# Attention block with a spline FFN: key tile 0 of the later query tiles transposed by VectorE and moved by DMA

## The chip, the cores and the metric

One Trainium2 chip, one of its NeuronCores. The metric is the device time in microseconds of one execution. A core has TensorE (PE; its weight loads are listed as PEld), VectorE (DVE), ScalarE (ACT), GpSimd (POOL) and SyncE (SP). In this kernel SP computes nothing and issues most DMAs. Every engine works through its own instructions in the order of the program and waits on semaphores for the others.

## The reference

A block on x of shape 4 x 512 x 512 in float32: a layer norm, attention with 16 heads of 32 (ALiBi bias over the keys, causal mask), and an FFN whose weights are splines of control points. Both branches read the normalized x and are added to x.

```
xn = layernorm(x)
q, k, v = xn@Wq + bq, xn@Wk + bk, xn@Wv + bv            # 16 heads of 32
scores = q k^T / sqrt(32) + slope[h] * (key - 511)       # causal mask, softmax over keys
ctx = softmax(scores) v;  attn = ctx @ Wo + bo
gate, up = xn @ gate_w^T, xn @ up_w^T                    # weights: cubic splines of control points
out = x + attn + (silu(gate) * up) @ down_w^T
```

## The kernel before, in words

The kernel has an attention part, until about 371 us of the profile, and an FFN part behind it; the change lies in the first. Attention runs over 64 **units** (b, hg, i): batch b of 4, head group hg of 4 (four heads each), query tile i of 4 (128 queries each). Unit i sees the key tiles 0 to i. One loop over n issues the parts of several units, staggered: step n computes the scores of unit n, normalizes unit n-1, transposes and moves unit n-2 (`LAG_SWAP`), and turns unit n-3 (`LAG`) on TensorE. Since each engine runs in program order, the order of the loop body is the order on each engine.

For a unit:
- `scores` (L889, TensorE) writes four heads into PSUM banks; tiles 0 and 1 share one set of banks and are issued together when i is 0.
- `minima` (L907, VectorE) adds the bias table `dist` and finds each row's minimum; `exponentials` (L923, ScalarE) makes p and its sums; `normalize` (L936 reciprocal on VectorE, L938 scaling on POOL) divides p by the sums.
- The value product needs p with keys on the partitions. There are two ways to it. **Key tile 0**: `turn` (L951) transposes four heads on TensorE into PSUM, and ScalarE copies them to `pT` (L952). **Key tiles 1 to i**: `swap` (L964) transposes blocks of 32 x 32 on VectorE into `blocks`, and `move` sends the blocks to their partitions with four DMAs on SP's queue (L974), into `moved`. A block transpose leaves keys in steps of 4, so that k is stored in stepped order for the key tiles from 1 on (L844), while key tile 0 keeps its order (L843).
- `values` (L994), once per head group at n % 4 = 3, multiplies: four matmuls (four heads) for each key tile; key tile 0 from `pT` with 512 queries, key tile c from `moved` with 512 - 128c. `moved` has one buffer.

Between these lie the projections (`project` L826 for q and k, `value` L864, `proj` L490 for the output), placed at steps by the tables `items`, `small` and `early`, which also place `load_turned` (the next batch's x, 1 MB), `keep_samples` (1 MB to DRAM, by way of a queue `later` that is emptied at the end of each step, by `flush`), and layer norm pieces. VectorE also builds the FFN's weights in attention: a list `terms` of multiplications and additions (L1135) is worked off by a credit per step, `TERMS`; the tables that a term reads are loaded by `loads` (two DMAs of 512 KB, later 256 or 320 KB), which also go through `later`.

The end of step n is, in this order: `swap` on VectorE, terms, `items` and `small`, then

```
            move()
            flush()
```

so that SP's queue holds what the step's items issue, then the moves, then the late loads and samples.

Of the kernel before, what the change touches and what calls it, by code (L numbers as in the profile page):

```python
# [18 lines left out]
P = 128  # L19
B, S, D, H = 4, 512, 512, 16  # L20
HD = D // H
# [9 lines left out]
NSLOT = 7  # L31
# [21 lines left out]
TERMS = (0.7, 1.4, 1.4, 0.7)  # L53
# [347 lines left out]
def block_kernel(  # L401
# [46 lines left out]
    lone = [keep.tile([P, S], F32, name="lone0")]  # L448
# [20 lines left out]
    dist = wp.tile([P, NB * (NB + 1) // 2, P], F32, name="dist")  # L469
# [34 lines left out]
    def keep_samples(b):  # L504
        nc.sync.dma_start(
            out=samples[b][1 : D + 1].rearrange("(c p) s -> p c s", p=P), in_=xnT[b]
        )
        nc.sync.dma_start(out=samples[b][:1], in_=lone[0][:1])
        nc.sync.dma_start(out=samples[b][D + 1 : D + NW], in_=lone[0][: NW - 1])
# [77 lines left out]
    with ExitStack() as att:  # L587
# [19 lines left out]
        nc.gpsimd.memset(lone[0], 0.0)  # L607
# [13 lines left out]
        for i in range(NB):  # L621
            for c in range(i + 1):
                shape, steps = dist[:, i * (i + 1) // 2 + c], [[1, P]]
                if c:
                    shape = shape.rearrange("p (r y) -> p r y", y=Q32)
                    steps = [[1, NB], [NB, Q32]]
                nc.gpsimd.iota(
                    shape,
                    pattern=steps,
                    base=1 - S + (c + NB - 1 - i) * P,  # L630
                    channel_multiplier=0,
                    allow_small_or_imprecise_dtypes=True,
                )
                if c == i:
                    nc.gpsimd.affine_select(
                        out=shape,
                        in_=shape,
                        pattern=[[-step, n] for step, n in steps],
                        compare_op=ALU.is_ge,
                        fill=NEG,  # L640
                        base=0,
                        channel_multiplier=1,
                    )

        spare = feat[0].rearrange("p c h s -> p (c h s)")
        loads, terms = {}, []

        def row_terms():  # L650
            size = NB * 2 * P
            place = lambda n: (spare[:, (2 * n + k) * size :][:, :size] for k in range(2))
            shaped = lambda a: a.rearrange("p (q x n) -> p q x n", q=NB, x=2)
            parts = [(c, w) for c in range(TAPS) for w in range(2)]

            def load(n, queue=nc.sync):
                c, w = parts[n]
                tab, own = place(n % 2)
                queue.dma_start(out=tab, in_=coef[c])
                queue.dma_start(out=own, in_=rowpts[c, w])  # L660

            for n, (c, w) in enumerate(parts):
                to = wT[:, :, 2 * w : 2 * w + 2, :]
                tmp = shaped(wd[:, w * size : (w + 1) * size]) if c else to
                tab, own = (shaped(a) for a in place(n % 2))
                terms.append((1.2, tmp, tab, own, ALU.mult))
                if n + 2 < len(parts):
                    loads[len(terms)] = lambda n=n: load(n + 2)
                if c:
                    terms.append((1.2, to, to, tmp, ALU.add))  # L670
            return [lambda: load(0, nc.sync), lambda: load(1, nc.sync)]

        def down_terms():
            size = 5 * P
            at = np.cumsum([0] + [P * (hi - lo) * P for _, lo, hi, _ in DOWN_STEPS])

            def part(n, k):
                _, lo, hi, _ = DOWN_STEPS[n]
                return spare[:, (n % 3 * 2 + k) * size :][:, : (hi - lo) * P]

            def load(*steps):
                for n in steps:
                    for k, source in enumerate((downtab, downpts)):
                        given = source[at[n] : at[n + 1]].rearrange("(p x) -> p x", p=P)
                        nc.sync.dma_start(out=part(n, k), in_=given)

            loads[len(terms) - 1] = lambda: load(0, 1, 2)
            terms.append((2.4,))
            for n, (kind, lo, hi, c) in enumerate(DOWN_STEPS):
                to = (dR if kind == "v" else dM)[:, lo:hi].rearrange("p a n -> p (a n)")  # L690
                tmp = wd[:, n % 2 * size :][:, : (hi - lo) * P] if c else to
                terms.append((0.8, tmp, part(n, 0), part(n, 1), ALU.mult))
                if n + 3 < len(DOWN_STEPS):
                    loads[len(terms)] = lambda n=n: load(n + 3)
                if c:
                    terms.append((0.8, to, to, tmp, ALU.add))
# [120 lines left out]
        def project(name, b, hg, parts=1):  # L817
# [3 lines left out]
            def go(part=0):  # L821
                if part == 0:
                    ps.append(ps_m.tile([P, S], F32, name="mm"))
                tokens = slice(part * size, (part + 1) * size)
                for c in range(NB):
                    nc.tensor.matmul(  # L826
                        ps[0][:, tokens],
                        lhsT=wsb[name][:, c, hg * P : (hg + 1) * P],
                        rhs=xnT[b][:, c, tokens],
                        start=(c == 0),  # L830
                        stop=(c == NB - 1),
                    )
                if part < parts - 1:
                    return
                o = qkp.tile([P, S], F32, name=f"{name}T")
                g = slice(hg, hg + 1)
                if name == "q":
                    nc.scalar.activation(
                        o, ps[0], AF.Identity, bias=bqs[:, g], scale=qs[:, g]
                    )  # L840
                else:
                    g1 = bcol[:, 1, g]
                    nc.scalar.activation(o[:, :P], ps[0][:, :P], AF.Identity, bias=g1)  # L843
                    nc.scalar.activation(  # L844
                        o[:, P:].rearrange("p (t r y) -> p t r y", r=NB, y=Q32),
                        ps[0][:, P:].rearrange("p (t y r) -> p t r y", r=NB, y=Q32),
                        AF.Identity,
                        bias=g1,
                    )
                qk[b, hg, name] = o  # L850
# [25 lines left out]

        units = [(b, hg, i) for b in range(B) for hg in range(NHG) for i in range(NB)]
        soft, pT, banks = {}, {}, {}
        moved = {}
# [17 lines left out]
        def minima(u):  # L897
            b, hg, i = u
            nk = (i + 1) * P
            own = dist[:, i * (i + 1) // 2 :][:, : i + 1].rearrange("p c k -> p (c k)")  # L900
# [41 lines left out]
        def turn(u):  # L942
# [3 lines left out]
            if i == 0:  # L946
                pT[b, hg] = tp.tile([P, NG, S], F32, name="pT")
# [6 lines left out]
        def swap(u):  # L954
# [4 lines left out]
            if i == 1:  # L959
                moved[b, hg] = tp.tile([P, NB, NSLOT, NG, Q32], F32, name="moved")  # L960
            at = slice(2 * i - 2, 3 * i - 2)
            own = tp.tile([P, NB, i, NG, Q32], F32, name=f"blocks{i % 2}")
            for c in range(i):
                nc.vector.transpose(  # L964
                    own[:, :, c].rearrange("p r j k -> p j r k"),
                    soft[u][0][:, :, (c + 1) * P : (c + 2) * P].rearrange(
                        "p j (r k) -> p j r k", k=Q32
                    ),
                )
            to = moved[b, hg]  # L970

            def move():
                for a in range(NB):
                    nc.sync.dma_start(  # L974
                        out=to[:, a, at].rearrange("p s j k -> p (s j k)"),
# [5 lines left out]
        def values(b, hg):  # L981
# [3 lines left out]
            swapped = moved.pop((b, hg)).rearrange("p a s j k -> p s a j k")  # L985
            for c in range(NB):
                if c:
                    w = swapped[:, 3 * c - 3 : c + 4 : 2]
                    part = lambda j: w[:, :, :, j]
                else:  # L990
                    w = pT.pop((b, hg))
                    part = lambda j: w[:, j]
                for j in range(NG):
                    nc.tensor.matmul(  # L994
                        ps[j * HD : (j + 1) * HD, c * P :],
                        lhsT=vals[b][:, c, hg * P + j * HD : hg * P + (j + 1) * HD],
                        rhs=part(j),
                        start=(c == 0),
                        stop=(c == NB - 1),
# [26 lines left out]
        for b in range(B):  # L1026
# [16 lines left out]
            if b + 1 < B:  # L1043
                for t in range(NB):
                    small[at + 8 + t].append(lambda b=b, t=t: norm_turned(b + 1, t))
                items[at + (4, 5, 4)[b]].append(lambda b=b: load_turned(b + 1))
# [8 lines left out]
        for b in range(B):  # L1055
            at = 4 * NHG * b
            items[max(at - 4, 0)].append(lambda b=b: later.append(lambda: keep_samples(b)))
# [37 lines left out]
        done, credit = 0, 0.0  # L1095

        for n in range(len(units) + LAG):
# [4 lines left out]
            if u and u[2] == 0:  # L1102
                if old:
# [18 lines left out]
            if old and not (u and u[2] == 0):  # L1122
# [9 lines left out]
            while done < len(terms) and credit > 0.0:  # L1132
                cost, *term = terms[done]
                if term:
                    nc.vector.tensor_tensor(*term)  # L1135
                done += 1
                credit -= cost
                if done in loads:
                    later.append(loads[done])
# [3 lines left out]
            flush()  # L1143
            if n >= 12:
# [15 lines left out]
    lone.append(latep.tile([P, S], F32, name="lone1"))  # L1160
# [3 lines left out]
    def set_up_moments():  # L1164
        for zeros in (lone[1], *edge):
# [223 lines left out]
```

## Time and profile before

| | us |
|---|---|
| median of three runs | 526.22 (524.68 to 528.7) |
| the profiled execution, its own time | 524.87 |
| its span, first to last instruction | 523.1 |
| TensorE busy | 502.9 (96%) |
| VectorE busy | 349.5 (67%) |
| ScalarE busy | 285.9 (55%) |
| POOL busy | 243.5 (47%) |
| granted TensorE clock, mean | 0.993 |
| turns L951, busy of 256 matmuls | 41.3 |
| block transposes L964, busy of 96 | 61.8 |

DMA moves 104.88 MB, 201 GB/s on average. The profile is one execution; a busy share is an average over stages with different limits. A row of its groups names line, engine, operation, output and input tile, shape and count, then busy time and mean duration, then the engine's idle time just before these instructions and what ended it. In the timeline, rows merge neighbours: a start, a duration, and how many instructions (an f32 matmul counts as two, a transpose on TensorE as one).

### The profile page before, as it was taken

How to read it: one execution, taken by the hardware profiler on the slowest of the kernel's cores; microseconds unless marked ns; L12 is line 12 of the kernel's file. 1: busy time of each engine (PE TensorE's matmuls, PEld its weight loads, DVE VectorE, ACT ScalarE, POOL GpSimd, SP SyncE). 2: the span in 40 equal slices, each digit the busy share in tenths (PEclk: the TensorE clock that was granted, in tenths of full speed). 3: DMA queues.
4: the chain of work that ended last, by engine and by line, in shares of the span. 5: the costliest groups of instructions: out<-in, count | busy, mean ns of one | idle time of the engine just before them, and what ended most of it. 6: DMA issues, size and time to landing. Idle time of an engine off the chain costs nothing.

```text
span 523.1 us, 11781 instructions
## 1 busy us (share of the span) xinstructions
PE 502.9 (96%) x4092; PEld 246.2 (47%) x4092; DVE 349.5 (67%) x991; ACT 285.9 (55%) x774; POOL 243.5 (47%) x441
## 2 busy tenths in 40 slices
PE   7999899999999999999998999989899999999997
PEld 5644344444444444444434444434335646746462
DVE  6169888588778649968976456583233774856836
ACT  2377757666457656755765666775014523634232
POOL 3024636647446583745866547574036233231310
PEclk9999999999999999999998999998999999999999
DMA  8926887975797587768773436786747555654344
GB/s 304 338 104 165 276 233 213 271 212 161 234 312 215 147 248 190 211 194 255 198 237 93 117 79 175 218 214 163 250 142 232 178 207 181 245 196 146 138 160 166
DMA packets 65051, 104.88 MB, mean 201 GB/s; under 512 B 10368, under 2 KB 34944, under 8 KB 64480
## 3 DMA queue, kind: packets, MB, share of 16 engines
q1 hardware_dynamic: 60384, 95.73, 60.1%
q0 software_dynamic: 4608, 8.40, 5.5%
q8 instruction: 32, 0.52, 0.4%
q14 instruction: 27, 0.22, 0.2%
HBM read 54.27 MB, written 23.70 MB: 149 GB/s over the span
## 4 chain that ended last, share of the span: by engine, by line
PE 81%; DVE 7%; DMA 6%; SPq 4%; issue 2%; ACT 0%; DVEq 0%
PE mm L826 18%; PE g L570 9%; PE mm L864 8%; PE s L889 7%; PE mm L490 7%; PE c L994 6%; PE o L1261 6%; PE mm L951 5%; DMA moved<-blocks 4%; PE o L1207 4%; SPq L974 3%; PE o L1278 3%; PE o L490 3%; DVE p L907 3%; DVE blocks L964 2%; PE o L570 2%
## 5 line engine op out<-in xcount | busy, mean ns | idle before, releaser
L938 POOL TENSOR_SCALAR p<-p,inv 128x128 f32<-128x128 f32 (+3 forms) x256 | 146.5, 585 | 157.1 <-DVE inv L936 131.7
L923 ACT ACTIVATE p<-p,low 128x128 f32<-128x128 f32 (+3 forms) x256 | 140.6, 553 | 32.2 <-DVE low L907 32.2
L907 DVE CUSTOM_DVE_ANT_0 p<-s,dist 128x128 f32<-128x128 f32 (+3 forms) x256 | 108.7, 485 | 69.2 <-PE s L889 69.0
L1183 POOL COPY made<-inner 128x512 f32<-128x512 f32 x64 | 38.8, 635 | 101.0 <-DVE inner L1182 96.8
L964 DVE STREAM_TRANSPOSE blocks<-p 128x512 f32<-128x512 f32 x96 | 61.8, 682 | 4.0 <-POOL p L938 2.8
L1175 ACT ACTIVATE act<-g 128x512 f32<-128x512 f32 x60 | 31.0, 603 | 58.9 <-PE g L570 58.6
L570 PE MATMUL g<-feat,wT 32*64 32x512 f32 x832 | 61.8, 592 | 0.0
L864 PE MATMUL mm<-wv,xnT 128*128 128x512 f32 x128 | 57.9, 594 | 1.4 <-ACT xnT L777 1.4
L826 PE MATMUL mm<-xnT,wq 128*128 128x512 f32 (+1 forms) x136 | 57.9, 568 | 0.9 <-DVE xnT L813 0.9
L826 PE MATMUL mm<-xnT,wk 128*128 128x512 f32 (+1 forms) x136 | 58.0, 569 | 0.2 <-ACT xnT L777 0.2
L952 ACT COPY pT<-mm 128x512 f32<-128x512 f32 x64 | 36.8, 580 | 31.1 <-PE mm L951 31.1
L889 PE MATMUL s<-kT,qT 32*128 32x512 f32 (+3 forms) x512 | 52.0, 474 | 0.5 <-DVE low L907 0.3
L923 ACT ACTIVATION_READ_ACCUMULATOR p<-p,low 128x1 f32 x256 | 48.6, 190 | 0.0
L951 PE MATMUL mm<-ident,p 128*128 128x128 f32 x256 | 41.3, 286 | 0.0
L951 PEld LDWEIGHTS mm<-ident,p 128*128 128x128 f32 x256 | 28.5, 142 | 26.2 <-issue 18.9
L490 PE MATMUL mm<-ctxT,wo 128*128 128x512 f32 x88 | 39.8, 595 | 0.0
L1182 DVE TENSOR_TENSOR inner<-g,act 128x512 f32<-128x512 f32 x40 | 24.9, 684 | 21.7 <-PE g L570 15.5
L570 PEld LDWEIGHTS g<-feat,wT 32*64 32x64 f32 x832 | 29.3, 131 | 20.7 <-issue 9.7
L555 POOL DMA_DIRECT2D table<-samples x64 | 36.8, 581 | 0.0
L889 PEld LDWEIGHTS s<-kT,qT 32*128 32x128 f32 x512 | 21.3, 188 | 32.4 <-issue 15.4
L826 PEld LDWEIGHTS mm<-xnT,wq 128*128 128x128 f32 x136 | 24.9, 190 | 24.0 <-issue 22.0
L994 PE MATMUL c<-moved,v 128*32 128x384 f32 (+2 forms) x384 | 25.6, 402 | 10.6 <-DMA moved<-blocks 7.0
(113 smaller groups left out, 619.9 us busy)
## 6 DMA issues: line engine op xcount, KB each, us to landing
moved<-blocks SPq DMA_DIRECT2D x64, 192.0 KB
moved<-blocks SPq DMA_DIRECT2D x64, 128.0 KB
feat<-table SPq DMA_DIRECT2D x16, 512.0 KB
inner<-made SPq DMA_DIRECT2D x32, 256.0 KB
table<-samples POOLq DMA_DIRECT2D x64, 88.0 KB, 3.6
xp<-in_xp_dram SPq DMA_DIRECT2D x16, 256.0 KB
feat<-in_coef_dram SPq DMA_DIRECT2D x8, 512.0 KB
feat<-in_rowpts_dram SPq DMA_DIRECT2D x8, 512.0 KB
```

The costliest lines, as they stand in the source:

```text
L490: nc.tensor.matmul(ps, lhsT=wsb["o"][:, c, r * P : (r + 1) * P], rhs=ctxT[b][:, c, :], start=(c == 0), stop=(c == NB - 1),)
L570: nc.tensor.matmul(ps[k][cols, :], lhsT=wT[rows, q, 2 * w + part, cols], rhs=feat[b][rows, q, part, :], start=(part == 0), stop=(part == 1),)
L826: nc.tensor.matmul(ps[0][:, tokens], lhsT=wsb[name][:, c, hg * P : (hg + 1) * P], rhs=xnT[b][:, c, tokens], start=(c == 0), stop=(c == NB ...
L864: nc.tensor.matmul(ps[0], lhsT=xnT[b][:, c, t * P : (t + 1) * P], rhs=wsb["v"][:, c, :], start=(c == 0), stop=(c == NB - 1),)
L889: nc.tensor.matmul(banks[b, hg][j][:, at : at + (k + 1) * P], lhsT=qk[b, hg, "q"][rows, k * P : (k + 1) * P], rhs=qk[b, hg, "k"][rows, : ( ...
L907: nc.vector.tensor_tensor_reduce(out=p[:, j, :nk], in0=ps[j], in1=own, scale=-SLOPES[hg * NG + j], scalar=BIG, op0=ALU.add, op1=ALU.min, a ...
L923: nc.scalar.activation(p[:, j, :nk], p[:, j, :nk], AF.Exp, bias=low[:, j : j + 1], scale=-1.0, accum_out=total[:, j : j + 1],)
L938: nc.gpsimd.tensor_scalar(p[:, j, :nk], p[:, j, :nk], inv[:, j : j + 1], 1.0, ALU.mult, ALU.mult)
L951: nc.tensor.transpose(ps[:, j, :], p[:, j, :P], ident)
L964: nc.vector.transpose(own[:, :, c].rearrange("p r j k -> p j r k"), soft[u][0][:, :, (c + 1) * P : (c + 2) * P].rearrange("p j (r k) -> p ...
L994: nc.tensor.matmul(ps[j * HD : (j + 1) * HD, c * P :], lhsT=vals[b][:, c, hg * P + j * HD : hg * P + (j + 1) * HD], rhs=part(j), start=(c ...
L1183: nc.gpsimd.tensor_copy(made[:, k], four[:, k])
```

## The change

- `turn` is done for query tiles 0 and 1 alone (`TURNED = 2`). For tiles 2 and 3, key tile 0 goes the way of the others: one block transpose more on VectorE for each, and moves of three and four key tiles in place of two and three.
- k is stored stepped for all key tiles, with one activation in place of two. The rows of `pT` are then in stepped order, so its product needs v's first tile in the same order: `stepped(b)` copies it with four DMAs into a free slot of the moved tile, once per batch, at the step behind the last value product of the batch before.
- `values` has five groups of four matmuls in place of four: `pT` with 256 queries and the stepped v, then key tiles 0 to 3 from the moved blocks with 256, 384, 256 and 128 queries. The moved tile is now one tile, `blocks`, kept for the whole of attention.
- `dist` needs 4 tiles in place of 10. The zero rows for `samples` are issued by POOL at the start from a small buffer, not by SP in `keep_samples`.
- `keep_samples` goes two steps later, behind the moves of query tile 3, and `load_turned` to step 6 of its batch (it was at 4, 5, 4). Loads for terms are gathered in `due` and issued only at the end of steps with n % 4 of 1 or 2; a term whose load has not been issued waits. `TERMS` gives 0.9 in place of 0.7 at two of four steps, and an empty term of 2.4 is gone.

```diff
-NSLOT = 7
+NSLOT = 9
+TURNED = 2
-TERMS = (0.7, 1.4, 1.4, 0.7)
+TERMS = (0.9, 1.4, 1.4, 0.9)
...
-                    g1 = bcol[:, 1, g]
-                    nc.scalar.activation(o[:, :P], ps[0][:, :P], AF.Identity, bias=g1)
                     nc.scalar.activation(
-                        o[:, P:].rearrange("p (t r y) -> p t r y", r=NB, y=Q32),
-                        ps[0][:, P:].rearrange("p (t y r) -> p t r y", r=NB, y=Q32),
+                        o.rearrange("p (t r y) -> p t r y", r=NB, y=Q32),
+                        ps[0].rearrange("p (t y r) -> p t r y", r=NB, y=Q32),
                         AF.Identity,
-                        bias=g1,
+                        bias=bcol[:, 1, g],
                     )
...
+        blocks = tp.tile([P, NB, NSLOT, NG, Q32], F32, name="moved")
+        def stepped(b):
+            rows = vals[b][:, 0].rearrange("(y r) (a d) -> r y a d", r=NB, a=NB)
+            for r in range(NB):
+                to = blocks[r * Q32 : (r + 1) * Q32, :, 1]
+                nc.sync.dma_start(out=to.rearrange("p a j k -> p a (j k)"), in_=rows[r])
...
-            at = slice(2 * i - 2, 3 * i - 2)
-            own = tp.tile([P, NB, i, NG, Q32], F32, name=f"blocks{i % 2}")
-            for c in range(i):
+            first = int(i < TURNED)
+            at = slice(3 * i - 4 + first, 4 * i - 3)
+            own = tp.tile([P, NB, i + 1 - first, NG, Q32], F32, name=f"blocks{i % 2}")
+            for c in range(first, i + 1):
...
+            parts = [(lambda j: blocks[:, hg, 1, j], slice(0, TURNED * P), lambda j: turned[:, j])]
             for c in range(NB):
+                i = max(c, 1 if c else TURNED)
+                w = swapped[:, 3 * i - 4 + c : 6 + c : 3]
+                parts.append((head(vals[b][:, c]), slice(i * P, S), lambda j, w=w: w[:, :, :, j]))
...
-                items[at + (4, 5, 4)[b]].append(lambda b=b: load_turned(b + 1))
+                items[at + 6].append(lambda b=b: load_turned(b + 1))
...
-            items[max(at - 4, 0)].append(lambda b=b: later.append(lambda: keep_samples(b)))
+            items[at + 4 if b else 1].append(lambda b=b: stepped(b))
+            items[max(at - 2, 0)].append(lambda b=b: later.append(lambda: keep_samples(b)))
...
-                if old:
+                if old and old[2] < TURNED:
                     turn(old)
...
-            if old and not (u and u[2] == 0):
+            if old and old[2] < TURNED and not (u and u[2] == 0):
                 turn(old)
...
+            if n % NB in (1, 2):
+                for load in due.values():
+                    load()
+                due.clear()
```

## Prediction

> **What bounds the kernel now.** I read the page first: busy shares, then the chain that ended last.
>
> ```profile
> PE 502.9 (96%) x4092; PEld 246.2 (47%) x4092; DVE 349.5 (67%) x991; ACT 285.9 (55%) x774; POOL 243.5 (47%) x441
> PE 81%; DVE 7%; DMA 6%; SPq 4%; issue 2%; ACT 0%; DVEq 0%
> ```
>
> TensorE (PE) is busy for 96%, yet a fifth of the chain lies elsewhere, with VectorE (DVE), a move's issue (SPq) and a DMA in it. So there are two paths of nearly equal length. Next the groups by shape: the work that is removed or multiplied.
>
> ```profile
> L951 PE MATMUL mm<-ident,p 128*128 128x128 f32 x256 | 41.3, 286 | 0.0
> L964 DVE STREAM_TRANSPOSE blocks<-p 128x512 f32<-128x512 f32 x96 | 61.8, 682 | 4.0 <-POOL p L938 2.8 <-DMA moved<-blocks 1.2
> L952 ACT COPY pT<-mm 128x512 f32<-128x512 f32 x64 | 36.8, 580 | 31.1 <-PE mm L951 31.1
> ```
>
> Then TensorE's own waits, longest total first:
>
> ```profile
> PE c L994 <- DMA moved<-blocks: 7.0, 6, 2.9
> ```
>
> The only wait that returns (6 times, 2.9 us at most) is the value product's wait for the moves. I therefore measure the loop by a **window**, one for each of the 16 value products: from the end of the score matmuls of query tiles 0 and 1 to the first c<-moved matmul. Window 4 on TensorE's timeline (start us, us, instruction):
>
> ```profile
> 105.15 0.94 PE L889 MATMUL s<-kT,qT 32*128 32x128 f32 x16
> 106.02 0.66 PE L951 MATMUL mm<-ident,p 128*128 128x128 f32 x4
> ...
> 109.95 0.60 PE L951 MATMUL mm<-ident,p 128*128 128x128 f32 x4
> 110.39 3.60 PE L826 MATMUL mm<-xnT,wk 128*128 128x512 f32 x8
> ...
> 114.77 0.66 PE L951 MATMUL mm<-ident,p 128*128 128x128 f32 x4
> ...
> 120.02 1.06 PE L994 MATMUL c<-pT,v 128*32 128x512 f32 x8
> 120.90 1.48 PE L994 MATMUL c<-moved,v 128*32 128x384 f32 x24
> 122.31 0.66 PE L951 MATMUL mm<-ident,p 128*128 128x128 f32 x4
> ```
>
> It runs from 106.02 to 120.90, 14.88 us without a gap: the **TensorE path**. The **move path** starts at the same instant; DVE and SP timelines:
>
> ```profile
> 108.33 1.30 DVE L964 STREAM_TRANSPOSE blocks<-p 128x512 f32<-128x512 f32 x2
> 109.56 0.14 DVE L936 RECIPROCAL inv<-sum 128x4 f32<-128x4 f32 x1
> 109.61 1.86 DVE L964 STREAM_TRANSPOSE blocks<-p 128x512 f32<-128x512 f32 x3
> ```
>
> ```profile
> 109.66 5.65 SPq L974 DMA_DIRECT2D moved<-blocks  x8
> ```
>
> Two transposes for query tile 2, three for tile 3, eight issues of about 0.62 us. By the trace's packet records tile 2's packets (1024 B) start 4.85 to 8.15 us into the window, tile 3's (1536 B) 7.70 to 12.03; the last move has landed at 12.42. The product needs tile 3's four moves for every key tile, so this path has 14.88 - 12.42 = 2.5 us to spare. That spare is what the change spends.
>
> **TensorE's side.** Of four turns a head group, those of tiles 2 and 3 go. The start of the next matmul shows what a turn costs the stream: 0.44 (109.95 to 110.39) and 0.49 us (0.59 before the stretch product), though the busy column says 41.3 / 64 = 0.65; I take the gaps. Ahead of the moves' arrival the pT part has 256 columns in place of 512: 120.02 to 120.90 is 0.88, so 0.44 goes. An ordinary window shrinks from 14.72 to 14.72 - 0.44 - 0.49 - 0.44 = 13.35. Behind the arrival four matmuls of 256 columns are added: 0.44 plus some 0.03 for each extra group (122.31 - 120.90 = 1.41 for 768 columns), so 1.41 becomes 1.88, **+0.47, 16 times, +7.5 us**. If TensorE alone decided, 16 x (1.37 - 0.47) = 14.4 us would be gained.
>
> **The move path's side.** One transpose more for tile 2 and one for tile 3, each 61.8 / 96 = 0.62 to 0.64 us; DVE reaches both in order, so whatever stands between (reciprocal, term) is later too. The moves stay four DMAs a tile with as many packets, but of 1536 in place of 1024 B and 2048 in place of 1536 B. From first to last packet, 512-B moves take 2.4 to 3.6 us, 1024-B ones 2.9 to 3.4 where alone, 1536-B ones 4.1 to 4.9. So tile 2 grows by 0.7 to 1.5; I take 0.9. For tile 3 no move of 2048 B exists; lower bound 0 (four issues at 0.62 already pace 1.9 us; a gain is excluded, each packet being longer), upper 4.4 x 4/3 - 4.4 = 1.5; I take 1.0, the step from 1024 to 1536 B, the nearest row. In window 4 the two queues follow each other: 12.42 + 0.62 + 0.9 + 1.0 = **14.9 us** against TensorE's 13.35. The move path decides, with a wait of 1.5 us at the product; a term of 1.2 us between the transposes still hides behind tile 2's packets.
>
> [...]
>
> **The windows, before and after** (TensorE's timeline; after is the longer path):
> - Ordinary, 2, 3, 4, 7, 10, 12, 14: 15.27 + 15.87 + 14.88 + 15.98 + 14.88 + 14.73 + 14.72 = 106.3; after 7 x 14.9 = 104.3. **-2.0.** The waits of 0.96 and 1.07 in windows 3 and 7 came from `keep_samples`: its 1 MB stood in SP's queue right ahead of tile 3's moves (issued 90.00 and 179.32), and now goes two steps later, behind them.
> - 1 and 6, with over 2 us of small DVE work between the transposes: 16.78 + 14.73 = 31.5. In window 6 tile 3's packets begin at 9.15; less 0.35 for a shorter term, plus 1.24, plus 4.7 + 1.0 + 0.4 is 16.1; window 1 is like it, less its 1 MB of loads now behind the moves. After 32.0. **+0.5.**
> - 5 and 9, with four output projections (21.8 each): TensorE decides. **-2.7.**
> - 8, 13, 15, 16, with little TensorE work between, already on the move path: 8 and 13 grow by 0.62 + 0.9 + 1.0 = 2.5 each; in 15 and 16 tile 3's transposes wait for an output projection, so 0.62 + 1.0 each. **+8.2.**
> - 11: 18.94 with the 2.9 us wait behind `keep_samples` and a late xnT; after 14.9. **-4.0.**
>
> These cancel: 0.0.
>
> **The clock.** The granted clock falls after long waits:
>
> ```profile
> 260.00:280.00 20.00, 17.10 (x95) 7.79 (x97) 13.25 (x39) 12.70 (x38) 14.84 (x26) 0.93 0.64 191
> 340.00:360.00 20.00, 17.46 (x87) 7.70 (x86) 12.62 (x38) 12.14 (x38) 15.29 (x29) 0.91 0.72 194
> ```
>
> The last three columns are clock, DMA share, GB/s. Half clock came for 3.41 us after the waits of 2.90 and 2.54, not after 1.73; one such stretch costs 1.6 us (c, turn and s after 276.44 take 1.96, 1.12, 1.59 in place of 1.50, 0.66, 0.94). One goes with window 11, one may come with 2.6 us in windows 1 or 6: 0. [...]
>
> **Edits at nothing.** ScalarE loses 32 copies of 0.58 and one of two kT activations: idle there, 55% busy; nothing gained. DVE's 32 transposes are 20.6 us more; 69.0 us of waiting for s cover them outside the windows; uncovered, all 20.6. The zero rows' eight issues (0.58 each, the rows of POOL's table copies) go from SP to POOL, which does nothing before its first normalization at 28.34; uncovered, 4.6 us. The stepped v copy is four issues per batch (2.5 us), ahead of tile 2's moves in windows 5, 9 and 13, but the wait for the previous product ends some 8 us before window 13; uncovered, 2.5 there. Loads of tables now follow tile 3's moves; terms are the same operations, finished two head groups earlier. `load_turned` comes up to two steps later; its readers wait for `rows` as it is (2.2 us in all); late, it would hold DVE and the next q product by a few us.
>
> **The sum.** 0.0 + 7.5 + 0 = +7.5 on the profiled execution of 524.87 (span 523.1 and 1.8 around it): 532.4. The median shown, 526.22, lies 1.35 above that execution, so **533.5**.
>
> **Rivals.**
> - *Bytes ride free* (the other side): the larger moves pace by their issues, and only the transpose is added, 13.0, so TensorE's 13.35 decides. Ordinary windows lose 1.55 x 7, 1 and 6 1.9 each, 8 and 13 1.9 each, 15 and 16 1.0 each, 11 1.55: -22, so 511.5. For it: 512 and 1024 B differ little (2.4 to 3.6 against 2.9 to 3.4), and median packets are short (65 ns at 1536 B, mean 97). Against: 1536 B takes over a microsecond longer. It beats the old time once the move path is under 14.4.
> - *Half of it*: growth 0.95 in place of 1.9. About 14 windows are 0.95 shorter, -13: 520.5; with the forecast's side of it up to 528.
> - *More of it*: 15.6, the upper bound, since DMA is busy 0.7 to 0.85 in most of attention: +10, and with waits of 2.2 some half clocks, up to 550.
> - *VectorE becomes the bound*: 17 to 22 us busy per group of 18 to 28 now; if every added transpose lies on the path, 546. Against: its wait for s, 69.0.
>
> That the change misses its purpose is excluded: in the instruction order half the L951 turns are gone and DVE has 128 transposes.
>
> **How the numbers follow.** Forecast (moves at 14.6 to 15.3, 529 to 540) 0.45; bytes free 0.13; half 0.20; more 0.17; VectorE 0.05. A tenth of a microsecond in the move path is 1.4 us, so the range runs 522 to 545, the forecast's own 529 to 540. A measurement tells about 1% (5.3 us) from nothing; faster: 0.13 and 0.02 of half, 0.15; same: 0.18 of half and 0.16 of the forecast's lower end, 0.34; slower: 0.51.
>
> **What would show it.** Right: PE's busy time down by some 15 to 20 us while its waits "c <- DMA moved" rise from 7 to 20 us or more, in nearly every ordinary window; tile 3's packets 5 us or longer; no wait behind `keep_samples` in windows 3, 7, 11. Wrong: ordinary windows near 13.4 without a wait; tile 3's packets as short as now; waits of s for DVE in place of those of c.

## The result, and the profile after

The changed kernel takes 579.12 us (median of 6 runs, 575.23 to 580.56), the kernel before 525.72 beside it: ratio 1.101, 95% interval 1.097 to 1.105. The forecast was 533.5, with a range of 522 to 545: the sign was right, the size was not. The profiled execution took 576.13 us; its span is 574.4, which is 51.3 more than before, and that is what the tables below split up.

Busy shares and the chain that ended last, profile after:

```profile
PE 516.5 (90%) x4092; PEld 247.7 (43%) x4092; DVE 369.2 (64%) x1023; ACT 268.5 (47%) x726; POOL 242.6 (42%) x441
PE 62%; DMA 18%; SPq 9%; DVE 8%; issue 3%; ACT 0%; DVEq 0%
```

VectorE has 19.7 us more (20.6 were worked out). TensorE has lost half of its turns and gained as many product matmuls, and its busy time, which the forecast had falling by 15 to 20 us, *rose* by 13.6 us: the same matmuls took longer. Its idle time went from 20.2 to 57.9 us. The chain lies for 27% in DMA and its issue, against 10% before. Groups (busy, mean ns of one | idle before them):

```profile
L972 DVE STREAM_TRANSPOSE blocks<-p 128x512 f32<-128x512 f32 x128 | 80.9, 680 | 9.6 <-DMA moved<-blocks 8.0
L1000 PE MATMUL c<-moved,v 128*32 128x256 f32 (+2 forms) x512 | 42.2, 484 | 38.0 <-DMA moved<-blocks 17.4
L898 PE MATMUL s<-kT,qT 32*128 32x512 f32 (+3 forms) x512 | 60.0, 483 | 8.6 <-DVE low L916 8.6
```

VectorE's transposes wait 8.0 us for moves (1.2 before): tile 1 of the next head group writes the buffer that tile 3's moves still read. The product now waits 38.0 us in all (10.6 before). The profile names the transfer that came last, so this is spread over several rows of TensorE's waits (us, times, longest):

```profile
PE c L1000 <- DMA moved<-blocks: 17.4, 7, 3.9
PE s L898 <- DVE low L916: 8.6, 5, 2.6
PE c L1000 <- DMA xt<-in_xT_dram: 8.5, 2, 6.2
PE c L1000 <- issue: 5.5, 2, 3.2
PE c L1000 <- DMA token<-by_token: 3.7, 2, 2.4
PE mm L864 <- DVE inv L945: 3.3, 1, 3.3
```

The second and the last row are all but new (0.3 us and none before): scores and a projection wait for *VectorE*. Window 4 again, TensorE, VectorE and SP (start, us):

```profile
117.91 0.94 PE L898 MATMUL s<-kT,qT 32*128 32x128 f32 x16
118.78 0.66 PE L960 MATMUL mm<-ident,p 128*128 128x128 f32 x4
...
132.26 0.64 PE L1000 MATMUL c<-pT,moved 128*32 128x256 f32 x8
134.30 0.96 PE L1000 MATMUL c<-moved,v 128*32 128x256 f32 x12 [1.40 <-DMA moved<-blocks]
```

```profile
121.09 1.89 DVE L972 STREAM_TRANSPOSE blocks<-p 128x512 f32<-128x512 f32 x3
122.91 1.18 DVE L1143 TENSOR_TENSOR wd<-feat 128x1024 f32<-128x1024 f32 x1
124.01 0.17 DVE L945 RECIPROCAL inv<-sum 128x4 f32<-128x4 f32 x1
124.09 2.46 DVE L972 STREAM_TRANSPOSE blocks<-p 128x512 f32<-128x512 f32 x4
```

```profile
123.05 7.62 SPq L979 DMA_DIRECT2D moved<-blocks  x8
```

TensorE reaches the moves 14.1 us into the window (13.6 in windows 3, 7 and 14) and the product starts at 15.5. By the packet records, tile 2's packets (1536 B) start 5.4 to 10.0 us into the window, tile 3's (2048 B) 9.2 to about 15.

The third thing is the clock. Windows view around the product of window 3, which waits 2.25 us until 110.39 (length, busy of PE, PEld, DVE, ACT, POOL; then clock, DMA share, GB/s):

```profile
107.64:111.06 3.42, 1.17 (x20) 0.52 (x20) 3.22 (x11) 2.67 (x7) 3.42 (x8) 1.00 0.89 225
111.06:114.47 3.41, 3.41 (x29) 2.18 (x22) 1.71 (x3) 0.94 (x3) 3.37 (x5) 0.50 0.97 316
114.47:117.88 3.41, 3.41 (x9) 1.24 (x7) 0.00 (x0) 0.59 (x1) 3.05 (x5) 1.00 1.06 411
```

Attention has 58.0 us of such half clock in 11 stretches (6.8 us in 2 before); the mean clock is 0.949 (0.993).

The forecast's sum beside what the traces show, in us of the profiled executions (from the same instants as there; window 16, which has no scores ahead of it, from its first turn):

| part | forecast | measured |
|---|---|---|
| ordinary windows 2, 3, 4, 7, 10, 12, 14 | -2.0 | +8.7 |
| windows 1 and 6 | +0.5 | +7.5 |
| windows 5 and 9 | -2.7 | -0.1 |
| windows 8, 13, 15, 16 | +8.2 | +12.8 |
| window 11 | -4.0 | -2.1 |
| from the first c<-moved to the next window, 15 times | +7.5 | +20.5 |
| ahead of window 1, and the FFN | 0 | +3.9 |
| sum | +7.5 | +51.3 |

### The profile page after: what moved, and what is told of

It reads as the page before. It is cut to its first block, busy times and chain, and to the rows that moved or that the text cites. A ratio compares the mean times of both kernels' runs of the same rounds, so it can differ in the third digit from the quotient of the medians.

```text
span 574.4 us, 11703 instructions
## 1 busy us (share of the span) xinstructions
PE 516.5 (90%) x4092; PEld 247.7 (43%) x4092; DVE 369.2 (64%) x1023; ACT 268.5 (47%) x726; POOL 242.6 (42%) x441
## 4 chain that ended last, share of the span: by engine, by line
PE 62%; DMA 18%; SPq 9%; DVE 8%; issue 3%; ACT 0%; DVEq 0%
PE mm L828 15%; DMA moved<-blocks 10%; PE g L569 8%; SPq L979 7%; PE c L1000 6%; PE o L1273 5%; PE s L898 4%; PE mm L864 4%; PE o L1219 4%; PE mm L491 3%; DVE blocks L972 3%; PE o L491 3%; PE o L1290 3%; PE mm L960 3%; DVE p L916 2%
## 5 line engine op out<-in xcount | busy, mean ns | idle before, releaser
L947 POOL TENSOR_SCALAR p<-p,inv 128x128 f32<-128x128 f32 (+3 forms) x256 | 143.0, 571 | 203.4 <-DVE inv L945 184.5
L972 DVE STREAM_TRANSPOSE blocks<-p 128x512 f32<-128x512 f32 x128 | 80.9, 680 | 9.6 <-DMA moved<-blocks 8.0
L1000 PE MATMUL c<-moved,v 128*32 128x256 f32 (+2 forms) x512 | 42.2, 484 | 38.0 <-DMA moved<-blocks 17.4
L898 PE MATMUL s<-kT,qT 32*128 32x512 f32 (+3 forms) x512 | 60.0, 483 | 8.6 <-DVE low L916 8.6
L864 PE MATMUL mm<-wv,xnT 128*128 128x512 f32 x128 | 60.9, 619 | 4.3 <-DVE inv L945 3.3
L1000 PEld LDWEIGHTS c<-moved,v 128*32 128x32 f32 x512 | 20.9, 133 | 62.2 <-issue 49.2
L898 PEld LDWEIGHTS s<-kT,qT 32*128 32x128 f32 x512 | 26.7, 189 | 43.2 <-issue 19.2
L1194 DVE TENSOR_TENSOR inner<-g,act 128x512 f32<-128x512 f32 x40 | 24.9, 684 | 21.7 <-PE g L569 10.7
L864 PEld LDWEIGHTS mm<-wv,xnT 128*128 128x128 f32 x128 | 24.3, 201 | 33.2 <-issue 28.1
L828 PEld LDWEIGHTS mm<-xnT,wk 128*128 128x128 f32 x136 | 25.5, 190 | 29.5 <-issue 28.2
L569 PEld LDWEIGHTS g<-feat,wT 32*64 32x64 f32 x832 | 27.9, 131 | 22.2 <-issue 12.2
```

What stands on the lines that cost most here:

```text
L569: nc.tensor.matmul(ps[k][cols, :], lhsT=wT[rows, q, 2 * w + part, cols], rhs=feat[b][rows, q, part, :], start=(part == 0), stop=(part == 1),)
L828: nc.tensor.matmul(ps[0][:, tokens], lhsT=wsb[name][:, c, hg * P : (hg + 1) * P], rhs=xnT[b][:, c, tokens], start=(c == 0), stop=(c == NB ...
L864: nc.tensor.matmul(ps[0], lhsT=xnT[b][:, c, t * P : (t + 1) * P], rhs=wsb["v"][:, c, :], start=(c == 0), stop=(c == NB - 1),)
L898: nc.tensor.matmul(banks[b, hg][j][:, at : at + (k + 1) * P], lhsT=qk[b, hg, "q"][rows, k * P : (k + 1) * P], rhs=qk[b, hg, "k"][rows, : ( ...
L947: nc.gpsimd.tensor_scalar(p[:, j, :nk], p[:, j, :nk], inv[:, j : j + 1], 1.0, ALU.mult, ALU.mult)
L972: nc.vector.transpose(own[:, :, c - first].rearrange("p r j k -> p j r k"), soft[u][0][:, :, c * P : (c + 1) * P].rearrange("p j (r k) -> ...
```

## The experiments

Two theories at first. **P**: the longer move path, and the half clock that its waits bring. **L**: the new places of the loads starve VectorE's terms. Each ratio is to the kernel before, run beside that run. The last three columns come from the traces: windows 1 to 15, the 14 stretches between them, and half clock in attention. From here on a window starts at the modelled end of the score matmuls, so each is 0.07 us shorter than by the prediction's instants.

| run | us | ratio to before, 95% | windows | between | half clock |
|---|---|---|---|---|---|
| before | 525.72 | | 239.2 | 71.0 | 6.8 |
| changed | 579.12 | 1.101 (1.097-1.105) | 264.2 | 91.2 | 58.0 |
| turned4 | 527.88 | 1.008 (1.005-1.012) | 234.9 | 76.5 | 10.2 |
| old_place | 588.34 | 1.120 (1.111-1.129) | 272.1 | 97.7 | 81.9 |
| fill | 570.93 | 1.086 (1.078-1.093) | 266.9 | 81.7 | 30.7 |
| less_moved | 536.18 | 1.019 (1.012-1.026) | 232.1 | 85.1 | 27.3 |
| early_loads | 569.60 | 1.084 (1.078-1.091) | 258.4 | 86.2 | 51.2 |
| turned3 | 552.39 | 1.050 (1.043-1.057) | 247.6 | 81.6 | 34.1 |
| turned4_early | 523.40 | 0.997 (0.994-1.001) | 238.6 | 71.0 | 6.8 |
| before_keep | 518.35 | 0.987 (0.983-0.992) | 233.3 | 70.9 | 6.8 |
| early_fill | 563.11 | 1.074 (1.067-1.080) | 267.1 | 75.9 | 20.5 |
| less_moved_early | 530.31 | 1.013 (1.006-1.021) | 231.9 | 78.7 | 20.5 |
| two_queues | 607.31 | 1.157 (1.149-1.165) | 292.9 | 93.6 | 88.7 |

**turned4**: the change without its moves.

```diff
-TURNED = 2
+TURNED = 4
...
-            for c in range(NB):
+            for c in range(int(TURNED == NB), NB):
```

> TensorE turns key tile 0 of all four query tiles again and none of it is moved (moves of 64, 128 and 192 KB as before); everything else of the change stays: stepped keys, v's stepped copy, the placement of the large transfers. Theory P (the longer move path and the half clock that its waits bring are the 53 us): 522 to 530 us, the loop's windows 14.5 to 15 us and half clock in two stretches at most. Theory L (the placement of the loads starves VectorE's terms, and those waits make the loss): 540 to 555 us, with VectorE waiting 7 us or more for feat<-in_rowpts or feat<-in_downpts as in the changed kernel.

527.88: P. Nearly the whole loss goes with the moved tile. But L's wait is there all the same, in one place; TensorE's waits:

```profile
PE s L898 <- DVE low L916: 5.0, 2, 4.7
```

By the starts of its windows this run loses 6.2 us by the end of head group 1, hardly anything from there to head group 10 (5.9), and wins 4.7 back in 11.

**old_place**: the changed kernel with the old places of all loads.

```diff
-            items[max(at - 2, 0)].append(lambda b=b: later.append(lambda: keep_samples(b)))
+            items[max(at - 4, 0)].append(lambda b=b: later.append(lambda: keep_samples(b)))
...
-                    due[done] = loads[done]
+                    later.append(loads[done])
```

(and `load_turned`, `TERMS` and the empty term as before).

> The changed kernel with keep_samples, load_turned and the loads of the tables where they were before (issued in the step of the term that frees their buffer, keep_samples four steps ahead); key tile 0 of tiles 2 and 3 is still turned by VectorE and moved. Theory P: 570 to 582 us, the waits of the value product as in the changed kernel. Theory L: 545 to 560 us, VectorE's 15 us of waiting for tables gone and with it the waits of the score matmuls for VectorE (8.6 us) and the half clock behind them.

588.34, beyond both expectations: 9 us *worse* than the changed kernel. L as the main cause falls; the new places are on balance a help to the longer moves. Windows 3, 7 and 11, which have `keep_samples` ahead of the moves again, wait 6.2, 5.6 and 6.4 us.

**fill**: matmuls with zero weights keep TensorE busy ahead of the wait.

```diff
+                for j in range(NG * FILL if c == 0 else 0):
+                    nc.tensor.matmul(ps[...], lhsT=nothing, rhs=part(j % NG), start=False, stop=False)
```

> The changed kernel with twelve more matmuls (zero weights, 256 columns, about 1.6 us) between the part of the value product that needs no move and the part that waits for the moves. If the half clock is worth about 22 us of the loss, as 58 us of half-clock stretches against 7 before say, the stretches that start at this wait go: 558 to 570 us, mean clock 0.97 or more. If the half clock costs nothing because the moves rule anyway: 579 to 590 us, since windows 5, 9 and others without a long wait get the 1.6 us on top.

570.93, slightly over the range: 8.2 us saved. The moves land no earlier (window 3 is 15.85 us, 15.83 in the changed kernel), but what follows runs at full clock. The stretch from that product to the next window, first in the changed kernel, then in fill:

```profile
110.39:118.84 8.45, 8.45 (x61) 4.50 (x62) 2.35 (x3) 2.79 (x7) 7.09 (x10) 0.80 1.00 359
```

```profile
111.60:118.42 6.82, 6.82 (x61) 3.53 (x62) 2.35 (x3) 2.70 (x7) 6.78 (x10) 1.00 0.96 363
```

The same 61 matmuls, 1.63 us apart.

**less_moved**: every transpose and product, but smaller packets.

```diff
+            sent = slice(3 * i - 3, 4 * i - 3)
...
-                        out=blocks[:, a, at].rearrange("p s j k -> p (s j k)"),
+                        out=blocks[:, a, sent].rearrange("p s j k -> p (s j k)"),
...
-                w = swapped[:, 3 * i - 4 + c : 6 + c : 3]
+                w = swapped[:, 3 * i - 4 + max(c, 1) : 6 + max(c, 1) : 3]
```

> The changed kernel with all its transposes and products, but key tile 0 of tiles 2 and 3 isn't sent: the moves are 128 and 192 KB as before, and the product reads the slots of key tile 1 in its place, so that part of the result is left out. If the larger packets make the path longer (theory P by bytes): the moves land 1.5 to 2.5 us earlier, ordinary windows 13.4 to 14.2 us, little half clock, 535 to 550 us. If the two added transposes do (theory P by transposes): landing at most 1 us earlier, 565 to 575 us. Theory L: 570 to 580 us.

536.18: P by bytes. 64 KB less in each of eight moves a group is worth 43 us. Windows 12 and 14 are 13.40 us without a wait, the forecast's TensorE path; windows 3, 4 and 7 are 14.2 to 14.5, see below. Window 12, TensorE (the changed kernel's product waits 1.58 us there):

```profile
301.82 0.64 PE L1003 MATMUL c<-pT,moved 128*32 128x256 f32 x8
302.28 1.91 PE L1003 MATMUL c<-moved,v 128*32 128x256 f32 x32
```

**early_loads**: is late data on VectorE a third cause? In the changed kernel, window 1, VectorE stands still, and SP issued that load late, behind tile 3's moves and `token`:

```profile
56.17 0.17 DVE L945 RECIPROCAL inv<-sum 128x4 f32<-128x4 f32 x1
64.22 1.23 DVE L1143 TENSOR_TENSOR wd<-feat 128x1024 f32<-128x1024 f32 x1 [7.88 <-DMA feat<-in_rowpts_dram]
```

```profile
41.54 15.48 SPq L979 DMA_DIRECT2D moved<-blocks  x12
57.12 2.13 SPq L799 DMA_DIRECT2D token<-by_token  x4
59.29 0.36 SPq L658 DMA_DIRECT2D feat<-in_coef_dram  x1
59.70 0.43 SPq L659 DMA_DIRECT2D feat<-in_rowpts_dram  x1
```

In window 6 the wait is for `rows`, issued at 166.37 closely behind 1 MB of `load_turned` (164.54), and tile 3's transposes are queued behind it:

```profile
175.89 1.42 DVE L815 TENSOR_TENSOR xnT<-xnT,rows 128x512 f32<-128x512 f32 x2 [3.46 <-DMA rows<-token]
177.23 0.17 DVE L945 RECIPROCAL inv<-sum 128x4 f32<-128x4 f32 x1
177.32 2.46 DVE L972 STREAM_TRANSPOSE blocks<-p 128x512 f32<-128x512 f32 x4
```

```diff
-            if n % NB in (1, 2):
+            if n < 2 * NB or n % NB in (1, 2):
...
-                items[at + 6].append(lambda b=b: load_turned(b + 1))
+                items[at + (4, 5, 4)[b]].append(lambda b=b: load_turned(b + 1))
```

> The changed kernel, but in the first two head groups the loads of the tables are issued in the step that frees their buffer, and load_turned stands two, one and two steps earlier, as before the change. If late data on VectorE is a third cause beside the moves and the clock: the wait for feat<-in_rowpts (7.9 us) and for rows (4.9 us) go, the 6.9 us behind window 1 become 3 and windows 6 and 10 lose 3 to 6 us each, 562 to 571 us. If VectorE's waits only stood in for waits of the moves: 576 to 582 us.

569.60: a third cause, worth 9.5 us. Window 6 falls from 21.69 to 16.28, window 10 from 18.78 to 15.27, and the stretch behind window 1 from 9.82 to 5.51; windows 1 and 5 grow by 0.8 and 1.9.

**turned3**: only tile 3's key tile 0 is moved (`TURNED = 3`).

> TensorE turns key tile 0 of query tile 2 again; only tile 3's is moved (64, 128 and 256 KB). If packets are paced by bytes (tile 3's phase 5.9 us in place of 4.3, tile 2's 3.3 as before), tile 3's moves land about 14.2 to 14.8 us into an ordinary window, TensorE reaches the product at about 14.0, waits stay under 1 us and no half clock comes from them: 528 to 538 us. If the loss grows evenly with every piece moved: about 553 us.

552.39: the number of the second expectation, and the threshold of the first is not there; but the loss is not even. The ordinary windows did as expected (3, 4, 7, 12, 14 are 14.05 to 15.41, waits up to 1.2 us). The loss came in the windows that carry other large transfers or little TensorE work: 1, 2, 6, 8, 11, 13 and 15 sum to 116.0 us against 102.3 in turned4. That these had little spare, so that the first added bytes cost there, is how I read it; no run took their other loads away. TensorE's waits:

```profile
PE c L1000 <- DMA moved<-blocks: 22.7, 11, 4.9
PE s L898 <- DVE low L916: 6.4, 4, 4.1
```

**turned4_early**: turned4 with the early loads.

> TensorE turns all four (as in the run turned4) and the loads are early as in early_loads; keep_samples stays two steps later. turned4 lost 6.2 us by the end of head group 1 and won 4.7 in head group 11, so without the first: 520 to 523 us. If the early loads hold tile 3's moves instead: 525 to 529 us.

523.40, just over the first range: the loss of head group 1 goes (stretch behind window 1: 10.2 to 3.1), but window 2 grows from 16.2 to 19.0, so part of the gain is given back; with 1 inside its interval it can't be told from before.

**before_keep**: one line of the change alone, in the kernel before.

```diff
-            items[max(at - 4, 0)].append(lambda b=b: later.append(lambda: keep_samples(b)))
+            items[max(at - 2, 0)].append(lambda b=b: later.append(lambda: keep_samples(b)))
```

> The kernel before the change with keep_samples alone issued two steps later, behind tile 3's moves. If its 1 MB is what holds those moves in windows 3, 7 and 11 (waits of 0.96, 1.07 and 2.90 us and one half-clock stretch): 519 to 522 us. If another load takes its place there: 525 to 528 us.

518.35, a little under the first range and the fastest version here. SP now issues the 1 MB behind the moves, and the product of window 11, which waited 2.90 us, finds them there:

```profile
264.97 3.33 SPq L974 DMA_DIRECT2D moved<-blocks  x4
268.34 0.61 SPq L505 DMA_DIRECT2D samples<-xnT  x1
```

```profile
271.19 1.06 PE L994 MATMUL c<-pT,v 128*32 128x512 f32 x8
272.46 1.50 PE L994 MATMUL c<-moved,v 128*32 128x384 f32 x24 [0.20 <-issue]
```

Windows 3, 7 and 11 are 14.66, 14.66 and 16.19 (15.80, 15.91 and 18.87 before). One half-clock stretch goes with window 11; another comes behind window 1, whose wait is now 2.04 us.

**early_fill, less_moved_early**: early_loads with the fill, and with the smaller moves.

> early_loads with the twelve zero-weight matmuls of the run fill ahead of the moves' wait. early_loads waits there in nearly every window (43 us in all) and has 55 us of half clock; its stretches behind the product are 9 us longer than at full clock. If the clock is a cost of its own that adds to the late loads: 557 to 562 us with under 25 us of half clock. If the two overlapped in the runs fill and early_loads: 566 to 572 us.

563.11, a microsecond over the first range: the clock's 6.5 us add to the 9.5 of the loads nearly in full.

> less_moved (key tile 0 of tiles 2 and 3 not sent, the slots of key tile 1 read in its place, so part of the result is left out) with the early loads of early_loads. If late data is separate from the bytes: 536 - 9 = 525 to 530 us, windows 1, 2 and 6 shorter by 8 together. If data was late only because the moves filled the queue: 533 to 538 us.

530.31, at the edge of "separate": 5.9 us less than less_moved, though the intervals of the two ratios overlap.

**two_queues**: bytes, or SP's issuing?

```diff
-                    nc.sync.dma_start(
+                    (nc.scalar if i == NB - 1 else nc.sync).dma_start(
```

> early_loads with tile 3's four moves issued by ScalarE in place of SyncE. If the moves are paced by their bytes through the 16 shared engines (1 MB in 5.9 us): ordinary windows stay at 15.3 to 16 us, 564 to 575 us. If SyncE's issues and its limit of eight open transfers pace them (the fourth issue comes 1.2 us after the third in place of 0.65): windows 14.3 to 15 us, 545 to 560 us.

607.31, worse than both expectations. Windows 4 and 12 are 16.2 and 16.4 (15.8 and 15.3 in early_loads), though in window 12 the last issue comes 10.1 us in instead of 10.8: the second issuer did not shorten the moves there, so SP's issues didn't set them. (The eight open transfers are in the traces: in the changed kernel SP's 478 transfers take eight semaphores strictly in turn, and 445 of them wait, before they are issued, on the semaphore that they then use.) The 607 itself has two causes that this run does not separate. First, ScalarE issues the moves between its own instructions, and its exponentials wait behind them (43.5 us in six waits put down to the moves). Window 4, ScalarE:

```profile
135.59 4.85 ACTq L979 DMA_DIRECT2D moved<-blocks  x4
140.55 0.61 ACT L932 ACTIVATE p<-p,low 128x384 f32<-128x384 f32 x1 [4.51 <-DVE inv L945]
```

Second, where SP has other loads, these no longer stand behind the moves but are issued beside them. Window 3, where ScalarE's issues start at 103.03; SP, then TensorE:

```profile
102.52 0.54 SPq L658 DMA_DIRECT2D feat<-in_coef_dram  x1
103.11 1.04 SPq L659 DMA_DIRECT2D feat<-in_rowpts_dram  x1
104.20 2.13 SPq L506 DMA_DIRECT2D samples<-xnT  x1
```

```profile
108.24 0.64 PE L1000 MATMUL c<-pT,moved 128*32 128x256 f32 x8
118.30 3.64 PE L1000 MATMUL c<-moved,v 128*32 128x256 f32 x32 [9.42 <-DMA moved<-blocks]
```

## Why the prediction was right or wrong

The runs, as a ladder: 579.1; the loads early, 569.6 (-9.5); then the added bytes not sent, 530.3 (-39.3); then TensorE's turns back, and with them the added transposes and the fifth group of the product gone, 523.4 (-6.9). Of the 39.3, the traces put 26.5 into windows 1 to 15 and 7.5 into the stretches between them.

The steps that failed, in the prediction's terms: the larger moves were priced by the ordinary window, and two terms were put at nothing, the clock ("0") and the loads' new places. The sum gave +7.5 and the profiles show +51.3. The forecast's own price of the added bytes, 533.5 - 511.5 = 22 us, came to 39.3; the loads cost 9.5, and the clock 6.5 to 8.2 by the two fills. (The sum is also off by 0.2: 532.4 + 1.35 is 533.75.)

- **Two paths, and the move path takes over: right.** TensorE's path is 13.6 us in windows 3, 7 and 14 (13.35 worked out), it waits in nearly every window, and the extra group costs 0.43 to 0.46 us where the clock is full (0.47).
- **"For tile 3 ... I take 1.0", "tile 2 ... 0.9": mis-sized.** Where they can be told from other packets, tile 3's take, from first to last, 5.3 us in window 12, 5.8 in window 3 and 5.9 in turned3's window 12: 0.9 to 1.5 more than 4.4, from about what I took to the *upper* end; tile 2's take 4.5, 1.2 more. The rows that I had said so already: 512 KB in 3.3 us is 159 GB/s, 768 KB in 4.4 is 179; at 179, 1 MB takes 5.9. Ordinary windows came to 15.2 to 15.9 where nothing else intervened (3, 4, 7, 12, 14), in place of 14.9: the rival "more of it" had this part (15.6). Of the 10.7 us that the row of ordinary windows is off, 6.7 lie in windows 2 and 10 (17.6 and 18.9 by the forecast's instants). Window 2 was no ordinary one: tile 3's packets began 10.5 us into it before the change, against 7.70 in window 4. In window 10 scores wait 2.6 us for VectorE and the product waits for nothing.
- **"A term of 1.2 us between the transposes still hides behind tile 2's packets": wrong without the bytes.** In less_moved, windows 3 and 4, tile 3's transposes start 5.25 us into the window and its packets at 9.0, 0.5 after tile 2's have ended; the moves land at 14.2 to 14.5 and not at 13.0. So the rival "bytes ride free" (511.5) had the wrong price as well: with the bytes gone the kernel takes 536, and 530 with the loads early.
- **"The clock ... 0": the step that failed in kind.** I allowed for one stretch won, with window 11, and one lost, at a wait of 2.6 us in window 1 or 6, and for none at the ordinary windows' 1.5. Ordinary waits came to 1.4 to 2.3 us, and 11 stretches came. TensorE was busy for 47.1 us of them, so at most 23.6 us of matmul time were lost (3.2 before); part of this lies beside moves that are late anyway, and the two fills save 8.2 and 6.5 us, net of what they cost where no wait was. The saving is all in the stretches between the windows (9.5 and 10.3 us); the windows get longer.
- **"Edits at nothing ... by a few us": 9.5 us, most of it in windows 6 and 10 and behind window 1.** I named the risk and priced it at zero. What counted was not the terms but what stands behind them in VectorE's order: tile 3's transposes, and minima that free the banks of the next scores. That hits the path under discussion.
- **"5 and 9 ... TensorE decides. -2.7": wrong.** They stayed where they were (-0.1). TensorE's own path did get shorter: 20.5 us each in less_moved, without a wait. With the larger moves the product waits 0.68 and 1.33 us.
- **Windows 8, 13, 15, 16**: +12.8 for +8.2. In 13 tile 3's packets take 7.5 us, until near 357: POOL's `table<-samples` runs beside them from 352.5, and a 512 KB load behind them on SP's queue (`feat<-table`, issued at 352.06) from 354.2. The forecast had nothing for a neighbour that a later landing meets.
- **`keep_samples`: right**, and the one part that a run shows to pay: its waits in 3, 7 and 11 are gone in turned4, and alone it makes the kernel 1.3% faster.
- Smaller steps: no run tests ScalarE's copies alone; its busy time fell by 17.4 us, and no gain shows. POOL was not idle ahead of 28.34, as I read it, but from 5.4 us on; the zero rows had room all the same.

The terms are nearly additive: early loads are worth 9.5 us with the added bytes and 5.9 without, the fill 8.2 and, with early loads, 6.5. What stays open: how much of the bytes' 39 us is clock, since no run held the clock and left everything else alone (by TensorE's busy time at half clock, 36.4 us in early_loads and 18.8 in less_moved_early, at most 8.8), and why window 2 grows in turned4_early.

## What to carry to other kernels

Price a larger transfer at the rate of the largest size that the trace shows, as the upper end, and not only by the step between two smaller ones (here 5.9 us at the 179 GB/s of 768 KB, where 5.3 to 5.9 came); and once the sum crosses into "the transfer decides", add what a returning wait does to the clock (6.5 to 8.2 us here, by the two fills) and to every neighbour in the same queue (9.5 us by the early loads). A path with spare in its ordinary stages may have none in those that carry other loads: look at the spare of each stage, not of the ordinary one. When a change bundles an order of transfers with something else, try the order alone: here it was the only part that a run showed worth keeping.

## What the runs showed of the hardware

- In the traces of the kernel before and of the changed kernel the half-clock stretches of the attention part last 3.41 or 6.83 us and start on one grid of 3.413 us, within 0.01 (the changed kernel's first and last start, 59.86 and 418.26, lie 105 steps apart); the totals in the table of the runs are whole steps too, from 6.8 (2) to 88.7 (26). A cell is one step of this grid. The same wait came out both ways: 2.25 us in window 3 lies in one cell (107.64 to 111.06) and is followed by half clock; 2.25 us in window 14 is split by a cell's border at 377.30 and is not. Of the changed kernel's 11 drops, 8 follow a cell with 1.86 us or more of idle TensorE; 3 follow one with only 0.65 to 0.76, and one cell with 2.08 brought none, which stays open.
- In window 3 the order within one queue helped, but did not shield. With the table loads and the 1 MB of samples issued behind tile 3's moves on SP's queue, the product waits 2.3 us (early_loads); with the same transfers beside them from two queues, 9.4 us (two_queues, where ScalarE's stops may have a part). Yet in early_loads, too, the packets of what is issued behind start 1.3 us before tile 3's last one (105.19 and 106.45; in the changed kernel 108.45 and 109.72).
